# A Mamba stack with experts on one core: squares at the slot's end, powers moved, two banks for transposes, one for outputs

## The chip, the cores and the metric

The kernel runs on one core of a Trainium2 chip. The metric is the time of the kernel on the device in microseconds (us); lower is better. The core has five engines that work side by side, each through its own list of instructions in order: TensorE (PE in the profile, with PEld for its weight loads), VectorE (DVE), ScalarE (ACT), GpSimd (POOL) and SyncE (SP), which here issues most of the transfers. They wait for one another only where data or buffers ask for it.

## The reference

The input x has 8 sequences of 512 tokens with 128 channels, all in float32. A modulated LayerNorm is followed by four Mamba-2 layers, a gated residual, a second modulated LayerNorm, and a mixture of 8 experts (two per token) with a shared expert:

```python
h = _layernorm(x) * (1 + ca) + sa
for l in range(4):                      # Mamba-2 layer
    zxbcdt = rmsnorm(h) @ Wi            # z, xBC, dt
    xBC = silu(causal conv of 4 taps)   # xs, Bm, Cm
    dt = softplus(dt + dtb)
    hs = hs * exp(dt * A) + dt * xs * B ; y = hs @ C + D * xs
    h = h + rmsnorm(y * silu(z)) @ Wo
x = x + ga * rmsnorm(h)
h = _layernorm(x) * (1 + cb) + sb
x = x + gb * moe(h)                     # rmsnorm, router, top 2 of 8, plus shared expert
```

## The kernel before

The scan over tokens is done in chunks of 128. A *unit* is one sequence in one layer (32 units, `U`), an *item* is one chunk of a unit (128 items, `NI`, four to a unit). One loop over t runs all of it as a software pipeline. In slot t each stage works on another item; the slots of the loop are the order in which every engine gets its instructions, since the schedule inside is written by hand (`tc.manual_schedule`). For item i the stages are, with the slot in which they run and the engine:

- `decay_rows` (slot i-4, DMA), `decay_diff` and `decay_mask` (slot i-3, GpSimd, L793 and L798), `decay_exp` (slot i-2, ACT, L809): the decay matrix dV of the chunk, 128 x 1024;
- `transposes` (slot i-2): PE transposes the inputs into a PSUM bank called ptx (L828), and ACT copies them to xT (L830); `weigh` (slot i-1): GpSimd scales xT to xd and xe (L836, L839);
- `gram` (slot i-1): PE multiplies B and C (L848) into the last columns of the bank in which the next item's transposes land; `mix` (slot i): DVE multiplies dV by it (L852);
- `state_out` (slot i): PE, from the carried state (L861, L870); `state_decay` on GpSimd (L886), `state_next` on DVE (L895, L902);
- `chunk_out` (slot i+1): PE (L910, L920); `gate` (slot i+1): DVE multiplies by silu(z) to g (L932); `square` (slot i+1): ACT squares g for the norm (L936);
- `project_out` (slot i+2): PE sums the squares (L947) and projects g (L951) into a PSUM bank po that two items share; `out_scale` (slot i+2, odd i): DVE forms the mean (L958), GpSimd raises it to -1/2 (L959); `out_add` (slot i+3, odd i, so an even slot): DVE adds both chunks to the residual h (L967).

Sixteen slots ahead the same loop prepares the units: `project_x`, `project_z` and `project_dt` on PE (L638, L644, L682), four convolution taps per block of channels (ACT L650, then DVE L660 three times), `silu` on ACT in every fourth slot with a table load before and after it (L672, L673, then L809), and softplus on DVE (L706 to L740). `renorm` makes the next layer's input: squares on ACT (L155), a GpSimd power (L149, L150), scaling (hn, L203), transposes (L208) and a copy (hT, L210).

[...] Before, three serve the projections, one ptx, two py and two po.

When the last layer of a pair of sequences is done, `rejoin(g)` takes them (group g of four) through the final norm, the residual, the second LayerNorm, the second norm and the router. It is a generator: each `yield` ends a piece. In the drain, from slot 112 on, it is stepped twice in a slot. `mean_squares` squares on ACT and `power` takes the result to -1/2: on GpSimd in one instruction for groups 0 and 1 (`on_pool`), on DVE by a first guess from the bits and three Newton steps, 11 instructions, for groups 2 and 3. At its end each group has 16 scatters (GpSimd indirect DMAs, L488) that send rows to the experts' lists. After the loop, the shared expert (`serve`, L557, L535, with ACT's L524 and L528) is interleaved with the pieces that are left; then 39 expert tiles follow, and the final sums.

Of the kernel before, what the change touches and what calls it, by code (L numbers as in the profile page):

```python
# [11 lines left out]
ALU = mybir.AluOpType  # L12
AX = mybir.AxisListType
PSUM = bass.MemoryType.PSUM
# [10 lines left out]
def adaln_mamba_moe(  # L25
# [27 lines left out]
    nc = tc.nc  # L53
# [239 lines left out]
    def power(v, name, on_pool):  # L293

        n = v.shape[1]
        y = small.tile([P, G2], F32, tag="py", name=f"py{name}")[:, :n]
        if on_pool:
            nc.gpsimd.tensor_tensor(y, v, mhalf[:, :n], ALU.pow)
            return y
        t = small.tile([P, G2], F32, tag="pt", name=f"pt{name}")[:, :n]  # L300
        nc.vector.tensor_single_scalar(t.bitcast(I32), v.bitcast(I32), 1, ALU.arith_shift_right)
        nc.vector.tensor_scalar(y.bitcast(I32), t.bitcast(I32), -1, 0x5F3759DF, ALU.mult, ALU.add)
        for _ in range(3):
            nc.vector.tensor_mul(t, y, y)
            nc.vector.scalar_tensor_tensor(t, t, -0.5, v, ALU.mult, ALU.mult)
            nc.vector.scalar_tensor_tensor(y, t, 1.5, y, ALU.add, ALU.mult)
        return y

    def mean_squares(h, eps, name, on_pool):
        n = h.shape[1]  # L310
        ss = small.tile([P, G2], F32, tag="pss", name=f"pss{name}")[:, :n]
        for j in range(n):
            nc.scalar.activation(unread, h[:, j, :], AF.Square, accum_out=ss[:, j : j + 1])  # L313
            if j % NC == NC - 1:
                yield
        v = small.tile([P, G2], F32, tag="pv", name=f"pv{name}")[:, :n]
        nc.vector.tensor_scalar(v, ss, 1.0 / DM, eps, ALU.mult, ALU.add)
        return power(v, name, on_pool)

    def rejoin(g):  # L320
# [17 lines left out]
        mine = slice(b0 % 2 * NC, b0 % 2 * NC + n)  # L338
        h, xt = (v[b0 // 2].rearrange("p b s d -> p (b s) d")[:, mine] for v in (hp, xp))
        on_pool = g < 2  # L340
        rs = yield from mean_squares(h, 1e-5, f"F{g}", on_pool)
        yield
        for j in range(n):
            nc.scalar.activation(h[:, j, :], h[:, j, :], AF.Copy, scale=rs[:, j : j + 1])
# [14 lines left out]
            yield  # L359
        v = small.tile([P, G2], F32, tag="pv", name=f"pvL{g}")[:, :n]  # L360
        nc.vector.tensor_scalar_add(v, mv[:, :, 1], 1e-5)
        rs = power(v, f"L{g}", on_pool)
        if on_pool:
            yield
# [9 lines left out]
        for k in (2, 1):  # L374
            for t, m in both(k):
                nc.vector.tensor_tensor(h[:, t, :], h[:, t, :], m, ALU.mult if k == 2 else ALU.add)
            yield
        rs = yield from mean_squares(h, 1e-8, f"G{g}", on_pool)
        yield

        while scatters and scatters[0][0] in held.get(len(rowpools), [])[:-1]:
# [2 lines left out]
        rows = [rowpools[-1].tile([P, G2, RW], F32, tag=f"row{c}", name=f"row{c}_{g}")[:, :n] for c in range(2)]  # L384
        for j in range(n):
            nc.scalar.activation(rows[0][:, j, :DM], h[:, j, :], AF.Copy, scale=rs[:, j : j + 1])  # L386
            if j % NC == NC - 1:
                yield
        for c in range(2):
            nc.scalar.activation(rows[c][:, :, DM + 1], tok[:, :n], AF.Copy, bias=float(c * T + b0 * L))  # L390
        for i, b in enumerate(seqs):
# [94 lines left out]
    def scatter(to, of, ix, group):  # L486

        i = nc.gpsimd.indirect_dma_start(  # L488
            out=to, out_offset=bass.IndirectOffsetOnAxis(ap=ix, axis=0), in_=of, in_offset=None
        )  # L490
        tc.declare_no_dep(i.ins, group=group, reason="the rows that they write are distinct")
        tc.add_to_no_dep_group(group, i.ins)
# [80 lines left out]
    with ExitStack() as actx:  # L573
# [6 lines left out]
        w3 = actx.enter_context(tc.tile_pool(name="w3", bufs=3))  # L580
        df = actx.enter_context(tc.tile_pool(name="df", bufs=6))
        rows = actx.enter_context(tc.tile_pool(name="rows", bufs=3, space=bass.MemoryType.DRAM))
        psX = actx.enter_context(tc.tile_pool(name="psX", bufs=1, space=PSUM))
        psY = actx.enter_context(tc.tile_pool(name="psY", bufs=2, space=PSUM))
        psO = actx.enter_context(tc.tile_pool(name="psO", bufs=2, space=PSUM))

        U = NL * B
        NI = U * NC
# [345 lines left out]
        def square(i):  # L934
            sqs[i] = wk.tile([P, NB, Q], F32, tag="sq", name=f"sq{i}")
            nc.scalar.activation(sqs[i], gs[i], AF.Square)  # L936
# [18 lines left out]
        def out_scale(i):  # L955
            if i % 2:
                rs = small.tile([P, 2], F32, tag="rg", name=f"rg{i}")
                nc.vector.tensor_scalar(rs, po[i // 2][:, 2 * DM : 2 * DM + 2], 1.0 / DI, 1e-5, ALU.mult, ALU.add)  # L958
                nc.gpsimd.tensor_tensor(rs, rs, mhalf[:, 0:2], ALU.pow)  # L959
                po[i // 2] = po[i // 2], rs  # L960

        def out_add(i):
            if i % 2:
                pp, rs = po.pop(i // 2)
                for c in range(2):
                    b, s = i // NC % B, i % NC - 1 + c
                    nc.vector.scalar_tensor_tensor(  # L967
                        hs[b][:, s, :], pp[:, c * DM : (c + 1) * DM], rs[:, c : c + 1], hs[b][:, s, :], ALU.mult, ALU.add
                    )

        def item(i):
            return 0 <= i < NI

        def unit(v):
            return 0 <= v < U
# [17 lines left out]
        for t in range(-NC * LEAD - EARLY, NI + 4):  # L993
            p = t + NC * LEAD
            drain = p >= NI
            if p == 5 - EARLY:
                gens["small"] = load_small()
            if p == 0:
                gens["experts"] = prepare_experts(df)
            if p == 7 - EARLY:  # L1000
                gens["lists"] = clear_lists()
            if t == NI - LEAD * NC + 2:
                for k, w in enumerate((sw1, sw2.rearrange("(k p) o -> p k o", p=P))):
                    w12.append(wip.tile([P, NPROJ], F32, tag="Wi", name=f"ws{k}")[:, :FH])
                    dst = w12[k] if k == 0 else w12[k].rearrange("p (k o) -> p k o", o=DM)
                    nc.sync.dma_start(dst, w)
            for g, seqs in enumerate(sets):
                if t == NC * (U - B) + NC * (seqs[-1] + 1) + 2:
                    gens["pairs", g] = rejoin(g)
            v, j = divmod(p, NC)  # L1010
            vc, jc = divmod(p - 1, NC)

            if (p + 2 * NC) % (NC * B) == 0 and unit(p // NC + 2):
                load_weights((p // NC + 2) // B)
            if p % (NC * B) == NC and unit(v):
                scale_weights(v // B)
            if p == NC:
                nc.scalar.activation(negA, negA, AF.Exp)
                nc.scalar.mul(negA, negA, -1.0)
            if (p + EARLY) % NC == 0 and 0 <= (p + EARLY) // NC < B:  # L1020
                gens[(p + EARLY) // NC] = enter((p + EARLY) // NC)
            if t % NC == 3 and unit(t // NC - 1) and t // NC - 1 + B < U:
                gens[t // NC - 1 + B] = renorm(t // NC - 1)

            if item(t + 4):
                decay_rows(t + 4)
            vz, jz = divmod(p - 5, NC)
            if jz == 0 and unit(vz):
                silu(vz)
            if item(t + 2):  # L1030
                decay_exp(t + 2)

            if item(t):
                state_out(t)
            if item(t - 1):
                chunk_out(t - 1)
            if item(t):
                state_decay(t)
            if item(t + 1):
                weigh(t + 1)  # L1040
            if drain and scatters and item(t + 3):
                scatter(*scatters.pop(0)[1:])
            if item(t):
                mix(t)
            if item(t - 3):
                out_add(t - 3)
            if item(t):
                state_next(t)
            if drain:
                step_pairs()  # L1050
            if item(t - 1):
                gate(t - 1)
                square(t - 1)
            if item(t - 2):
                project_out(t - 2)
            if item(t + 1):
                gram(t + 1)
            if item(t + 2):
                transposes(t + 2)
            if item(t + 3):  # L1060
                decay_diff(t + 3)
                decay_mask(t + 3)
            if unit(vc):
                conv_tap(vc, jc, 1)
            if item(t - 2):
                out_scale(t - 2)
            if unit(vc):
                conv_tap(vc, jc, 2)
                conv_tap(vc, jc, 3)
                px.pop((vc, jc))  # L1070
            for key in list(gens):
                if not step(gens[key]):
                    del gens[key]
            if drain and routed:
                serve()
            group_stages(p, ((sums_a, 7),))
            if j == 1 and unit(v):
                project_dt(v)
            group_stages(p, ((softplus_a, 2), (softplus_b, 3), (softplus_c, 5), (softplus_d, 6), (sums_b, 7)))
            if unit(v):  # L1080
                project_x(v, j)
                conv_first(v, j)
            if j == 0 and unit(v - 1):
                project_z(v - 1)

# [244 lines left out]
```

## Time and profile before

| | |
|---|---|
| median of 3 runs | 1150.12 us (1149.14 to 1151.19) |
| the profiled execution | 1149.32 us, of it the span 1146.8 us |
| items 0 to 112 (starts of L852) | 94.26 to 744.24 us |
| drain and rest of the Mamba part | 744 to about 880 us |
| last group's norm and router, shared expert | 880 to 937 us |
| last scatters | 937 to 957 us |
| expert tiles | 961 to 1117 us |

How to read it: the profile is of one execution. "Busy" of an engine is the time that its instructions took; a group of instructions is a source line with an engine, and its row ends with the idle time of the engine just before them and what ended it. The costliest groups are L793 on POOL (128 times 1905 ns), L852 on DVE (128 times 1211 ns), L660 on DVE (384 times 745 ns) and L809 on ACT (128 times 1051 ns). The starts of consecutive instructions of one engine can overlap their durations a little[...].

The small operations that the change moves take: L936 square 414 ns (x128), L959 power 716 ns (x64), L967 addition 343 ns (x128, two in a row start 260 ns apart), L298 power of 8 columns 1.64 us (x6), L848 300 ns (x256), L947 256 ns (x512).

### The profile page before, as it was taken

How to read it: one execution, taken by the hardware profiler on the slowest of the kernel's cores; microseconds unless marked ns; L12 is line 12 of the kernel's file. 1: busy time of each engine (PE TensorE's matmuls, PEld its weight loads, DVE VectorE, ACT ScalarE, POOL GpSimd, SP SyncE). 2: the span in 40 equal slices, each digit the busy share in tenths (PEclk: the TensorE clock that was granted, in tenths of full speed). 3: DMA queues.
4: the chain of work that ended last, by engine and by line, in shares of the span. 5: the costliest groups of instructions: out<-in, count | busy, mean ns of one | idle time of the engine just before them, and what ended most of it. 6: DMA issues, size and time to landing. Idle time of an engine off the chain costs nothing. (4 is left out here: it accounts for less than half of the span.)

```text
span 1146.8 us, 21570 instructions
## 1 busy us (share of the span) xinstructions
PE 964.2 (84%) x7130; PEld 730.3 (64%) x7130; DVE 856.5 (75%) x2084; ACT 761.1 (66%) x1641; POOL 855.9 (75%) x937
## 2 busy tenths in 40 slices
PE   3666899989999889999998999879664994999995
PEld 1234666766677667666666676657453673988882
DVE  2767888798988988988889888887764652666653
ACT  3676888888898788888978887876534741333320
POOL 6858889798898898988988988989666163555550
PEclk9777989999999999999999999986886896999997
DMA  6964536443253243343332434434201016877756
GB/s 154 235 164 158 181 100 188 132 133 110 85 162 110 87 140 109 108 128 107 121 110 87 141 109 125 134 91 131 86 26 37 6 47 156 227 225 224 222 153 224
DMA packets 134303, 151.19 MB, mean 132 GB/s; under 512 B 22569, under 2 KB 106697, under 8 KB 134193
## 3 DMA queue, kind: packets, MB, share of 16 engines
q1 hardware_dynamic: 127184, 137.91, 41.1%
q0 software_dynamic: 4672, 9.42, 2.5%
q10 hardware_dynamic: 2336, 2.50, 0.7%
q8 instruction: 56, 0.92, 0.3%
q14 instruction: 55, 0.44, 0.1%
HBM read 120.07 MB, written 29.71 MB: 131 GB/s over the span
## 5 line engine op out<-in xcount | busy, mean ns | idle before, releaser
L660 DVE SCALAR_TENSOR_TENSOR xbc<-px,cw,xbc 128x511 f32<-128x511 f32 (+2 forms) x384 | 286.2, 745 | 23.4 <-ACT xbc L650 16.3
L793 POOL TENSOR_TENSOR dV<-dV,cum 128x1024 f32<-128x1024 f32 x128 | 243.8, 1905 | 5.4 <-DMA dV<-crow 5.3
L852 DVE TENSOR_TENSOR dV<-dV,ptx 128x1024 f32<-128x1024 f32 x128 | 155.0, 1211 | 18.7 <-ACT xT L830 18.6
L798 POOL TENSOR_SCALAR_AFFINE_SELECT dV<-dV 128x1024 f32<-128x1024 f32 x128 | 142.6, 1114 | 9.3
L809 ACT ACTIVATE dV<-dV 128x1024 f32<-128x1024 f32 x128 | 134.5, 1051 | 14.5 <-POOL dV L798 14.1
L488 POOL DMA_INDIRECT yg<-y,ix x78 | 84.1, 1078 | 77.5 <-DVE y L1216 62.9
L936 ACT ACTIVATE sq<-g 128x256 f32<-128x256 f32 x128 | 53.0, 414 | 119.0 <-DVE g L932 105.1
L638 PE MATMUL px<-hT,Wi 128*128 128x512 f32 x192 | 103.6, 621 | 15.9 <-DVE xbc L660 14.5
L650 ACT ACTIVATE xbc<-px,cbias,cw 128x512 f32<-128x512 f32 x128 | 98.4, 769 | 27.2 <-PE px L638 25.6
L488 POOL DMA_INDIRECT xg<-row,ix x64 | 63.3, 989 | 50.4 <-ACT hds L524 29.7
L836 POOL TENSOR_TENSOR xd<-xT,dt 128x256 f32<-128x256 f32 x128 | 79.2, 619 | 27.3 <-ACT xT L830 26.9
L861 PEld LDWEIGHTS py<-xbc,st 128*128 128x128 f32 x384 | 59.8, 202 | 60.1 <-issue 47.3
L951 PE MATMUL po<-Wo,g 128*128 128x128 f32 x512 | 88.9, 297 | 0.0
L1198 ACT ACTIVATE hd<-ph,bs 128x256 f32<-128x256 f32 x78 | 32.7, 470 | 84.3 <-PE ph L1192 81.9
L920 PE MATMUL py<-dV,xd 128*32 128x128 f32 x2048 | 84.5, 284 | 0.0
L947 PEld LDWEIGHTS po<-ones,sq 128*128 128x128 f32 x512 | 67.6, 192 | 26.1 <-issue 23.4
L910 PEld LDWEIGHTS py<-xbc,dg 128*128 128x128 f32 x512 | 79.5, 202 | 7.0 <-issue 1.0
L848 PE MATMUL ptx<-xbc 128*128 128x128 f32 x256 | 55.8, 300 | 33.1 <-DVE dV L852 32.4
L910 PE MATMUL py<-xbc,dg 128*128 128x128 f32 x512 | 81.9, 285 | 0.0
L947 PE MATMUL po<-ones,sq 128*128 128x1 f32 x512 | 78.1, 256 | 0.5 <-ACT sq L936 0.5
L1192 PE MATMUL ph<-xt,w 128*128 128x256 f32 x312 | 75.9, 388 | 0.1
L1205 PE MATMUL pe<-w,hd 128*128 128x128 f32 x624 | 75.9, 275 | 0.0
(252 smaller groups left out, 2343.0 us busy)
## 6 DMA issues: line engine op xcount, KB each, us to landing
dV<-crow SPq DMA_DIRECT2D x128, 512.0 KB, 3.8
w<-in_L_ffn_ew_dram SPq DMA_DIRECT2D x78, 256.0 KB, 3.5
xg<-blank SPq DMA_DIRECT2D x64, 260.0 KB, 5.9
ecum<-crow SPq DMA_DIRECT2D x256, 48.0 KB, 3.4
rows<-xg SPq DMA_DIRECT2D x39, 130.0 KB, 3.3
b<-in_L_ffn_eb_dram SPq DMA_DIRECT2D x39, 64.0 KB, 3.8
x<-in_L_attn_x_dram SPq DMA_DIRECT2D x8, 256.0 KB, 6.9
md<-mods SPq DMA_DIRECT2D x8, 256.0 KB, 4.9
```

Of the source, the lines that this page charges most:

```text
L488: i = nc.gpsimd.indirect_dma_start(out=to, out_offset=bass.IndirectOffsetOnAxis(ap=ix, axis=0), in_=of, in_offset=None)
L638: nc.tensor.matmul(px[v, k][:, :L], Wi[l][:, c0 : c0 + P], hT[v], start=True, stop=True)
L650: nc.scalar.activation(xbc[v][:, k, :], px[v, k][:, :L], AF.Identity, bias=cbias[:, l, k : k + 1], scale=cw[:, l, k, KT - 1 : KT],)
L660: nc.vector.scalar_tensor_tensor(xbc[v][:, k, d:], px[v, k][:, : L - d], cw[:, l, k, KT - 1 - d : KT - d], xbc[v][:, k, d:], ALU.mult, ALU ...
L793: nc.gpsimd.tensor_tensor(dV[i], dV[i], cums[g][:, h0 : h0 + NH].unsqueeze(2).to_broadcast([P, NH, Q]), ALU.subtract)
L798: nc.gpsimd.affine_select(out=dV[i], in_=dV[i], pattern=[[0, NH], [1, Q]], compare_op=ALU.is_ge, fill=-200.0, base=0, channel_multiplier=-1,)
L809: nc.scalar.activation(dV[i], dV[i], AF.Exp)
L852: nc.vector.tensor_mul(Ms[i], Ms[i], pg.pop(i).unsqueeze(1).to_broadcast([P, NH, Q]))
L910: nc.tensor.matmul(py[i][:, k, :], dg[l][:, k, :], xbc[u][:, k, t], start=False, stop=True, skip_group_check=True,)
L920: nc.tensor.matmul(py[i][j * HD : (j + 1) * HD, k, :], xd[:, h, :], M[:, h, :], start=False, stop=True, skip_group_check=True,)
L947: nc.tensor.matmul(pp[:, 2 * DM + c : 2 * DM + c + 1], sq[:, k, :], ones[:, 0:1], start=(k == 0), stop=(k == NB - 1))
L951: nc.tensor.matmul(pp[:, c * DM : (c + 1) * DM], g[:, k, :], Wo[l][:, k, :], start=(k == 0), stop=(k == NB - 1))
```

## The change

It has six parts.

1. `square(t - 1)` is issued at the end of slot t, after the norm work and the convolution's first tap, in place of right after `gate(t - 1)`.
2. `out_add(t - 3)` is issued before `mix(t)` in place of after it.
3. The pool for ptx gets two banks in place of one, the pool for po one in place of two.
4. `out_scale` calls `power`, so the result goes to a tile of its own; for the items 125 and 127 (`i < NI - 4` is false) it runs on DVE.
5. For groups 0 and 1 of `rejoin` there is a `yield` between the DVE instruction that forms the variance and the GpSimd power, three times.
6. The second norm's squares (`rest` is n in place of NC) and its scaled rows are issued for all chunks of the group in one piece, in place of two.

```diff
-    def mean_squares(h, eps, name, on_pool):
+    def mean_squares(h, eps, name, on_pool, rest):
...
-            if j % NC == NC - 1:
+            if j % rest == rest - 1:
                 yield
         v = small.tile([P, G2], F32, tag="pv", name=f"pv{name}")[:, :n]
         nc.vector.tensor_scalar(v, ss, 1.0 / DM, eps, ALU.mult, ALU.add)
+        if on_pool:
+            yield
         return power(v, name, on_pool)
...
-        rs = yield from mean_squares(h, 1e-5, f"F{g}", on_pool)
+        rs = yield from mean_squares(h, 1e-5, f"F{g}", on_pool, NC)
...
         nc.vector.tensor_scalar_add(v, mv[:, :, 1], 1e-5)
+        if on_pool:
+            yield
         rs = power(v, f"L{g}", on_pool)
...
-        rs = yield from mean_squares(h, 1e-8, f"G{g}", on_pool)
+        rs = yield from mean_squares(h, 1e-8, f"G{g}", on_pool, n)
...
             nc.scalar.activation(rows[0][:, j, :DM], h[:, j, :], AF.Copy, scale=rs[:, j : j + 1])
-            if j % NC == NC - 1:
-                yield
+        yield
...
-        psX = actx.enter_context(tc.tile_pool(name="psX", bufs=1, space=PSUM))
+        psX = actx.enter_context(tc.tile_pool(name="psX", bufs=2, space=PSUM))
         psY = actx.enter_context(tc.tile_pool(name="psY", bufs=2, space=PSUM))
-        psO = actx.enter_context(tc.tile_pool(name="psO", bufs=2, space=PSUM))
+        psO = actx.enter_context(tc.tile_pool(name="psO", bufs=1, space=PSUM))
...
-                nc.gpsimd.tensor_tensor(rs, rs, mhalf[:, 0:2], ALU.pow)
+                rs = power(rs, f"g{i}", i < NI - 4)
...
+            if item(t - 3):
+                out_add(t - 3)
             if item(t):
                 mix(t)
-            if item(t - 3):
-                out_add(t - 3)
...
                 gate(t - 1)
-                square(t - 1)
...
                 project_x(v, j)
                 conv_first(v, j)
+            if item(t - 1):
+                square(t - 1)
             if j == 0 and unit(v - 1):
                 project_z(v - 1)
```

## The prediction

> **What bounds the kernel now.** I read the page first, then its busy time by stretches of 50 us, the list of waits, and the timeline of single stretches; the chain of waits reaches back only to 879 us.
>
> ```profile
> PE 964.2 (84%) x7130; PEld 730.3 (64%) x7130; DVE 856.5 (75%) x2084; ACT 761.1 (66%) x1641; POOL 855.9 (75%) x937
> ...
> 500.00:550.00 50.00, 46.50 (x399) 35.50 (x398) 43.09 (x91) 43.07 (x85) 44.17 (x49) 1.00 0.41 132
> ```
>
> Columns of the second line: stretch, length, then busy us of PE, PEld, DVE, ACT and POOL, clock, DMA share, GB/s. In the steady part all four engines are busy for 86 to 93%. No engine alone is the bound: a loop of waits between them is. The starts of L852 repeat every 8 items to 0.01 us: item 70 at 503.99, item 78 at 549.21. I call these 45.22 us a lap; items 0 to 112 (94.26 to 744.24) are 14 laps.
>
> ```profile
> ACT sq L936 <- DVE g L932: 105.1, 76, 6.3
> DVE py L895 <- PE py L870: 36.6, 31, 2.6
> PE ptx L848 <- DVE dV L852: 32.4, 31, 6.0
> DVE dV L852 <- ACT xT L830: 18.6, 15, 1.9
> DVE h L967 <- POOL rg L959: 17.6, 7, 7.8
> ```
>
> (Who waited for whom: us in total, times, longest.) The change aims at the first and third. But where does the lap turn? In the lap from 503.99 DVE waits in only four places for over 0.3 us: 1.42 for xT of item 71 (ACT, behind silu), 1.03 and 1.28 at L895 of items 73 and 77 (PE, behind the pz matmuls), 0.42 for st; 4.2 us in all. ACT's long waits for g are mostly slack: at 534.73 it had waited 2.50 us, but L760 two steps on could not begin before DVE's L758, which ends at 537.25, and began at 537.61. Removing that wait is worth 0.36 us there, not 2.5.
>
> The end is different:
>
> ```profile
> 817.38 1.65 POOL L298 TENSOR_TENSOR pyG<-pvG,mhalf 128x8 f32<-128x8 f32 x1 [6.04 <-DVE pvG L317]
> ...
> 872.29 0.16 DVE L958 TENSOR_SCALAR rg<-po 128x2 f32<-128x2 f32 x1 [2.10 <-PE po L951]
> 880.25 0.61 DVE L967 SCALAR_TENSOR_TENSOR h<-po,rg,h 128x128 f32<-128x128 f32 x2 [7.80 <-POOL rg L959]
> ...
> 878.84 0.70 POOL L1111 IOTA tiles<- 128x312 f32 x1
> 879.48 0.74 POOL L959 TENSOR_TENSOR rg<-rg,mhalf 128x2 f32<-128x2 f32 x1
> ```
>
> The last norm's input is ready at 872.45; its power stands on GpSimd behind ten scatters (865.80 to 878.59) and two iotas. The chain that ended last starts just there, at 879.54, with that power and then L967.
>
> **The skill.** The Trainium skill's PSUM page (PSUM — Partial Sum Buffer, "PSUM bank collisions raise a hardware error") counts accesses of two engines to one bank at once as a collision, reads with reads included, so software has to order them. The trace agrees: mix (L852) at 503.99 starts when the xT copy of the next item ends (503.96), though they read different columns of the bank. Its page Perfetto Trace Analysis, "Optimization Strategy", takes repeated gaps as a hint at too few buffers; L848's wait for mix fits, but the trace prices it at 32.4 us in 31 of 128 slots only. Trainium Architecture — The Big Picture, "Inside one NeuronCore", gives each engine its own stream; 10 scatters in front of a 0.74 us power show what order within a stream costs.
>
> **The change, part by part.** t is the slot.
>
> *Two banks for ptx.* gram(t+1) no longer waits for mix(t). In the lap this frees PE by 0.47 (510.34) and 1.00 us (534.02).
>
> *One bank for po, additions first.* In even slots project_out now waits for both out_adds. DVE pays nothing in busy time (0.52 us moves ahead of mix), but mix now stands behind the GpSimd power. At 503.61 that power (0.69) ends at 504.30: out_add runs 504.34 to 504.95, mix starts at 504.86 instead of 503.99, and L895, which before came after both, starts at 506.00 instead of 505.65: 0.35 us late. In slot 72 softplus holds DVE to 515.09, so out_add ends at 515.70; PE could issue L947 at 514.9 and waits 0.8 us.
>
> *Squares at the end.* ACT's order becomes exp, xT, norm work, conv, sq. No work is added. After silu (slots 1 mod 4) sq now stands behind hn (1.18 us) and conv (0.67): it ends about 506.1, where before it ended at 503.70, and PE's L947 at 504.74 waits for it, 1.4 us. This is the new wait that I expect everywhere after slots with hn or the renorm squares. Queued behind L947 on PE are L951, gram, transposes and px; ACT's xT and conv and GpSimd's xd wait for those.
>
> I lay the longest loop of the new order with the trace's start-to-start times: from xT(71) over hn, conv and sq to L947(68) 2.55; to L947(69) 3.98 (po to px 1.55, px 0.86, state 0.45, dg 0.54, py 0.58); gram, transposes, hT 2.97; to L947(70) 2.56 (through px and through the squares alike); to L895(73) 5.32 (px 1.65, px and pz 2.58, L870 and its end 1.09); DVE from there to L758's end 16.06, as now; ct, conv, sq to L947(74) 1.71; px 2.61; conv, sq and the silu block to xT(79) 7.55 (the block alone 6.46). The sum is 45.31. The loop through GpSimd (edec, 11.2 us of unbroken GpSimd work to the power, out_add, DVE to pz, L895(73), L758) comes to 45.2. So a lap goes from 45.22 to about 45.3: 14 laps, +1.3 us, and I take +2 with a first lap that pays the 0.35. Unknown: some 30 hops of which each may be off by 0.03, that is up to 0.9 us a lap either way. Bounds: below, the wait that DVE has now, 4.2 us, cannot all go; I take -0.9 a lap (-13 us); above, +0.9 (+13 us).
>
> *GpSimd's powers a piece later; rows and squares whole.* Only groups 0 and 1. In the drain GpSimd waited 2.15 us for pvF at 764.9 and 6.04 for pvG at 817.38, with xd, xe, the difference and the mask queued behind. In the new order these go first. From 744 to 812 GpSimd is busy 60.9 of 68 us, so at most the 2.15 can be won. From 812 to 850 the xd is not the only thing late: DVE's L895 of item 123 waited 3.3 us at 821.70 for PE behind phs, which waited for ACT's hds, which stood behind sq waiting for g; with sq last that goes. Against it, a DVE power (2.3 us) now precedes the indices in program order, so the 16 scatters, GpSimd's bound until 848, start only about 1 us earlier. I take -4 us for 744 to 850 (bounds +3 and -10).
>
> *Last powers on VectorE.* Two powers of 11 small operations on DVE; the row of the same code (880.97 to 883.22) says 2.25 us. For item 125 it costs up to 2.2 us in a stretch where DVE has no gaps (852 to 862), where GpSimd took 0.69: +1.5. For item 127: 872.45 + 2.25 = 874.7, out_add at 874.75 instead of 880.25: -5.5. What is late next is the first wait in the rest of the chain, ACT's squares of group 3 and PE's shared experts; PE has about 13 idle us between 874 and 894, so it can follow. Group 3 also needs fewer pieces, so one phs pair (1.03 us) less stands before pos, and goes under the 20 us of scatters. Together -5 (bounds 0 and -9).
>
> The experts after 961 us and the start are as before; I count them as nothing (the start's slots are bounded by the same engines, up to 2 us either way).
>
> **Sum.** +2 - 4 - 5 = -7 us against the profiled execution's 1149.3 (span 1146.8 and 2.5 around it); the median of the runs shown, 1150.1, lies 0.8 above it. -7 from the median gives 1143.
>
> **Rivals.**
> - *The lap does shrink (1130).* For it: 105 us of ACT waiting and 32 us of PE waiting vanish, and the slack I see may be used by a loop I have not laid. Against: DVE's own waits, the lap's true cost, have other releasers. At -0.8 a lap, -11, and -9 at the end: 1130.
> - *The single po bank binds (1155).* One mechanism: out_add, first on DVE, waits for the GpSimd power, and PE's project_out waits for out_add, so DVE, GpSimd and PE meet in every even slot. For it: GpSimd runs unbroken from 538.35 to 570.9, and its power ends after DVE's slot is free (504.30 against 503.99). Against: DVE waits there today for xT anyway. Priced at +1.0 a lap, +14, less 9 at the end: 1155. It decides from about +0.65 a lap on, where the end's 9 us are used up.
> - *Both cancel (1150).* +9 in the laps against -9 at the end; or the end's 5.5 us are taken back by PE's queue of shared experts, continuously busy from 894 on, and the laps stay at +2.
>
> **How the numbers follow.** Balanced laps with a shorter end, 1136 to 1147: 0.48. The shrinking lap: 0.18. The bank that binds: 0.23. Cancelling: 0.11. The time is that of the first, 1143, its own range 1136 to 1147. To leave out no more than two in ten the range runs to 1130 and to 1156. Within 0.2% (2.3 us of 1150.1, about what this kernel's measurement can tell from no change) lies the cancelling case: faster 0.66, same 0.11, slower 0.23.
>
> **What would show it.** Right: ACT's wait for g in front of sq and PE's L848 wait for mix nearly gone; new waits of PE's po matmul for sq and for L967's out_adds; DVE's out_add waiting for the power in even slots; lap near 45.3; pyG's 6 us gone; the last out_add 1 to 2 us after its scale, and the first expert tile's rows some 9 us closer to the last lap. Wrong: a lap under 44.8 or over 45.8, or an end chain that still starts with a wait of several us for GpSimd.

## The result, and the profile after

The changed kernel takes 1156.58 us (median of 6 runs, 1155.44 to 1160.49) against 1149.63 us of the kernel before in the same comparison: 1.0067 times, 95% interval 1.0050 to 1.0085, some 7 us slower. A later comparison gave 1.0055 (1.0038 to 1.0072). The profiled execution has a span of 1153.7 us, 6.9 more than the 1146.8 before. In lines after the change, numbers above about 310 are 2 to 4 higher: mix is L855, the square L939, the sum of squares L950, the addition L970, and the power of the outputs now stands in L298. The level of the kernel before differed between comparisons (1148 to 1170 us), so every ratio below is to runs of before in its own comparison.

The list of waits of the kernel after, with the same columns as before:

```profile
ACT xT L833 <- PE ptx L831: 100.4, 93, 5.8
PE po L950 <- ACT sq L939: 42.6, 43, 2.4
DVE py L898 <- PE py L873: 37.3, 28, 3.3
DVE h L970 <- POOL pyg L298: 34.7, 18, 13.9
POOL pyg L298 <- DVE rg L961: 21.3, 22, 8.1
PE po L950 <- DVE h L970: 15.4, 5, 7.9
ACT sq L939 <- DVE g L935: 10.3, 3, 6.2
```

Each wait at which the change aimed is gone or nearly gone: ACT's for g fell from 105.1 to 10.3 us, and TensorE's wait of 32.4 us for mix (L848, now L851) no longer stands in the list. They came back elsewhere. ACT now waits 100.4 us for the transposes, TensorE 42.6 us for the squares, and VectorE's wait for GpSimd's power ahead of the additions doubled from 17.6 to 34.7 us.

In the stretch in which the kernel before had 46.50 us of TensorE and 44.17 us of GpSimd:

```profile
500.00:550.00 50.00, 45.55 (x373) 34.13 (x371) 42.46 (x88) 41.82 (x82) 43.75 (x49) 1.00 0.42 135
```

All four engines are busy for 0.4 to 1.3 us less of the 50: the steady part did not become denser. The 6.9 us, by the starts of mix, after against before:

| stretch | before | after | difference |
|---|---|---|---|
| start to item 0 | 94.3 | 94.9 | +0.7 |
| items 0 to 16 | 100.8 | 102.6 | +1.8 |
| three laps with a change of layer (from items 16, 48, 80) | 46.82, 46.82, 46.81 | 47.67, 47.66, 47.66 | +2.5 |
| eight ordinary laps up to item 104 | 45.21 to 45.22 | 45.27 to 45.28, two of 46.37 and 45.70 | +2.0 |
| items 104 to 127 | 161.9 | 161.2 | -0.7 |
| item 127 to the last addition | 21.4 | 20.7 | -0.7 |
| from there to the end | 266.3 | 267.5 | +1.2 |

Six of the eight ordinary laps are at 45.27 to 45.28. The two others are longer: in the one of 46.37 the slot that is 1.1 us longer falls into a stretch with a lower clock (last section); in the one of 45.70 one slot is 0.4 us longer at full clock, and why is open.

Not every row can be put down to the change, since profiles of the same instructions differ. Items 0 to 16 take 100.8 to 103.2 us in the six profiles in which nothing of the change acts there (before, e7, b1, b3, b4, g3 of the next section), so +1.8 shows nothing.

For items 104 to 127, e7 is the measure: up to the last two powers it has the instructions of the kernel before, in the same order on TensorE, VectorE, ScalarE and GpSimd, and it takes 157.5 us, not 161.9. The 4.4 us arise before item 125 (134.9 against 139.3 us from item 104). The largest piece is the slot from item 121 to 122, 12.01 us before and 8.01 in e7: before, TensorE's granted clock was 0.53 from 796 to 803 us, and in e7 it was 1.00 over the same instructions.

From the last addition to the end, the kernel after takes 267.5 us in one profile and 264.0 in another (c1). The laps, in contrast, mostly repeat to about 0.1 us from profile to profile where no stretch of lower clock falls into them. So what is shown to be the change's is +2.5 us where the layer changes and +0.5 in the ordinary laps, 3.0 of the 6.9 us.

The laps were expected to cost 2 us and the end to gain 9. The laps cost more, most of it where the layer changes, and no gain at the end is to be seen.

### The profile page after: what moved, and what is told of

It is laid out like the page before. It is cut to its first block, busy times and chain, and to the rows that moved or that the text cites. A ratio compares the mean times of both kernels' runs of the same rounds, so it can differ in the third digit from the quotient of the medians.

```text
span 1153.7 us, 21642 instructions
## 1 busy us (share of the span) xinstructions
PE 955.2 (83%) x7130; PEld 730.4 (63%) x7130; DVE 866.5 (75%) x2106; ACT 763.3 (66%) x1641; POOL 857.8 (74%) x935
## 4 chain that ended last, share of the span: by engine, by line
PE 29%; DVE 28%; POOL 21%; DMA 8%; ACT 6%; issue 6%; SPq 2%; POOLq 0%; ACTq 0%; DVEq 0%
DVE xbc L663 10%; POOL dV L796 6%; PE pe L1209 5%; DVE dV L855 5%; DMA rows<-xg 4%; PE ph L1196 3%; POOL dV L801 3%; PE px L641 3%; POOL xg L491 2%; POOL pyg L298 2%; PE pz L647 2%; DVE g L935 2%; POOL xd L839 2%; POOL xe L842 2%; PE py L923 2%
## 5 line engine op out<-in xcount | busy, mean ns | idle before, releaser
L855 DVE TENSOR_TENSOR dV<-dV,ptx 128x1024 f32<-128x1024 f32 x128 | 155.0, 1211 | 2.8 <-ACT xT L833 2.8
L950 PE MATMUL po<-ones,sq 128*128 128x1 f32 x512 | 79.1, 258 | 60.6 <-ACT sq L939 42.6
L950 PEld LDWEIGHTS po<-ones,sq 128*128 128x128 f32 x512 | 69.2, 196 | 90.1 <-ACT sq L939 65.6
L833 ACT COPY xT<-ptx 128x384 f32<-128x384 f32 (+1 forms) x128 | 57.4, 448 | 100.5 <-PE ptx L831 100.4
L864 PEld LDWEIGHTS py<-xbc,st 128*128 128x128 f32 x384 | 61.5, 204 | 65.9 <-issue 41.9
L954 PE MATMUL po<-Wo,g 128*128 128x128 f32 x512 | 91.4, 303 | 0.0
L864 PE MATMUL py<-xbc,st 128*128 128x128 f32 x384 | 63.2, 290 | 18.2 <-DVE rg L961 9.4
```

The costliest lines, as they stand in the source:

```text
L855: nc.vector.tensor_mul(Ms[i], Ms[i], pg.pop(i).unsqueeze(1).to_broadcast([P, NH, Q]))
L864: nc.tensor.matmul(py[i][:, k, :], st[i - 1][:, k * P : (k + 1) * P], xbc[u][:, NB + 1, t], start=(k == 0), stop=True, skip_group_check=True,)
L950: nc.tensor.matmul(pp[:, 2 * DM + c : 2 * DM + c + 1], sq[:, k, :], ones[:, 0:1], start=(k == 0), stop=(k == NB - 1))
```

## The experiments

All start-to-start times are from the profiles, in us; "lap" is the usual ordinary lap, "layer" one with a change of layer.

| kernel | parts of the change in it | lap | layer | items 104-127 | ratio to before, 95% |
|---|---|---|---|---|---|
| before | none | 45.22 | 46.81 | 161.9 | 1 |
| after, again (c1) | 1 to 6 | 45.27 | 47.63 | 162.4 | 1.0055 (1.0038-1.0072) |
| e8 | 2 | 45.56 | 48.0 | 164.5 | 1.0119 (1.0085-1.0153) |
| e6 | 1 | 45.66 and more | 46.78 | 159.6 | 1.0027 (1.0009-1.0045) |
| e3 | 1, 2, 4, 5, 6 | 45.42 | 47.9 | 161.3 | 1.0087 (1.0052-1.0121) |
| e2 | 1, 3, 4, 5, 6 | 48.06 | 47.6 to 50.3 | 161.1 | 1.0284 (1.0264-1.0303) |
| e4 | 2, 3, 4, 5, 6 | 45.57 | 47.96 | 162.0 | 1.0066 (1.0037-1.0094) |
| g4 | 1, 2, 3 | 45.26 | 47.62 | 166.3 | 1.0079 (1.0054-1.0104) |
| e1 | 1 to 4 | 45.28 | 47.66 | 166.4 | 1.0143 (1.0113-1.0172) |
| e5 | 1 to 6, power of item 123 on DVE | 45.27 | 47.66 | 158.8 | 1.0119 (1.0097-1.0141) |
| g1 | 1 to 6, powers from item 109 on DVE | 45.27 | 47.62 | 173.2 | 1.0220 (1.0162-1.0279) |
| g5 | 1 to 6, part 2 not in the drain | 45.26 | 47.62 | 161.7 | 1.0075 (1.0048-1.0103) |
| e7 | 4 | 45.20 | 46.81 | 157.5 | 0.9985 (0.9968-1.0002) |
| b1 | 4, 5, 6 | 45.22 | 46.86 | 160.2 | 0.9993 (0.9978-1.0008) |
| b3 | 4, and 1 in the drain alone | 45.22 | 46.85 | 159.5 | 0.9975 (0.9954-0.9995) |
| b4 | 4, 5, 6, and 1 in the drain alone | 45.22 | 46.86 | 161.8 | 0.9992 (0.9977-1.0007) |
| g3 | as b3, power of item 123 on DVE | 45.20 | 46.80 | 161.4 | 0.9968 (0.9951-0.9984) |

e1, e2, e4 and e5 were compared together at a level of 1165.7 us for before, and g1, g3, g4 and g5 at 1169.6; the others at 1148 to 1150. In the profiles of the first two comparisons the stretch from the last addition to the end takes 284 to 295 us, in the others 263 to 268, while the laps agree. So laps are compared between all kernels, and times best within one comparison. The column of items 104 to 127 is one profile each; a difference of up to 4.4 us in it between two single profiles shows nothing.

**The squares back (e4), the order back (e2).** The first theory was that additions ahead of mix let mix wait for GpSimd (A); its rivals, that the rejoin's later powers (B) or the late squares (C) do the harm.

```diff
 gate(t - 1)
+square(t - 1)
...
-if item(t - 1):
-    square(t - 1)
```

> The changed kernel with the squares right after the gate again (part 1 undone). Theory C: the waits of TensorE's L950 for the squares (42.6 us in 43 slots) go, ordinary laps drop under 45.0 us, time about 1151. Theories A and B: ordinary laps stay within 0.2 of 45.3, the stall of item 126 stays, time within 2 us of 1156.6.

The lap grows by 0.3 us to 45.57, more than the 0.2 that A and B allowed, and it does not fall below 45.0. C is refuted: inside the change the late squares gain in the laps. The time does not show this gain: 1.0066, where the change itself had 1.0067 and 1.0055.

```diff
-if item(t - 3):
-    out_add(t - 3)
 if item(t):
     mix(t)
+if item(t - 3):
+    out_add(t - 3)
```

> The changed kernel with out_add after mix again, all else kept (part 2 undone). Theory A: the laps with a layer change go back from 47.66 towards 46.8 us, mix of item 126 no longer waits 14 us for the power of item 123 (it starts before 852 instead of 859.6), time 1150 to 1152. Against it, TensorE's po bank waits a little longer for the additions: up to +0.3 us a lap, and if this binds the time stays at 1156. Theories B and C: within 1.5 us of 1156.6.

The lap rises to 48.06, where A had expected it to stay within 0.3 us: a miss. It explains why the parts belong together. With one output bank, project_out cannot start before the additions are through: for 29 of the 30 pairs from items 40 and 41 to 98 and 99, TensorE's sum starts 0.15 to 0.43 us after the end of the additions. e6 below has the same order and the same late squares, but two output banks, and its shortest lap is 45.66. So behind mix the single bank costs up to 2.4 us a lap, and the order of part 2 takes 2.8 us off again. Only this order makes part 3 bearable.

**One part at a time (e8, e6, e3).**

> The kernel before with out_add ahead of mix and nothing else of the change: two output banks, early squares. Theory A (the order alone makes mix wait for GpSimd's power): laps with a layer change 47.9 instead of 46.8, items 112 to 120 in 51 to 53 us instead of 48, ordinary laps within 0.3 of 45.2; time 1.004 to 1.008 of before. The rival (the order costs only where late squares make the output sums, and with them the power, late): laps 45.2 and 46.8, items 112 to 120 in 48, time 0.999 to 1.001.

```diff
+if item(t - 3):
+    out_add(t - 3)
 if item(t):
     mix(t)
-if item(t - 3):
-    out_add(t - 3)
```

A holds, with the order as the only edit: ordinary laps +0.34, layers +1.2 (47.94 and 48.07; the first was 49.31). The time, +1.2%, is above the 0.4 to 0.8% that A had forecast. The waits between 240 and 740 us, first before, then e8, then after, show the exchange:

```profile
DVE dV L852 <- ACT xT L830: 12.0, 9, 1.4
DVE h L967 <- POOL rg L959: 1.3, 2, 0.6
```

```profile
DVE h L967 <- POOL rg L959: 17.6, 10, 1.8
```

```profile
DVE h L970 <- POOL pyg L298: 15.2, 11, 1.8
PE po L950 <- DVE h L970: 4.1, 2, 2.1
```

Before, VectorE waited 12.0 us for xT ahead of mix and hardly at all for the power. With the additions first it waits for the power instead, 15 to 18 us, and mix and all behind it wait too. The price is highest where GpSimd is late. VectorE in a slot at a layer change, first before, then after:

```profile
412.84 1.21 DVE L852 TENSOR_TENSOR dV<-dV,ptx 128x1024 f32<-128x1024 f32 x1
414.69 0.61 DVE L967 SCALAR_TENSOR_TENSOR h<-po,rg,h 128x128 f32<-128x128 f32 x2 [0.64 <-POOL rg L959]
```

```profile
418.52 0.61 DVE L970 SCALAR_TENSOR_TENSOR h<-po,pyg,h 128x128 f32<-128x128 f32 x2 [1.77 <-POOL pyg L298]
419.04 1.21 DVE L855 TENSOR_TENSOR dV<-dV,ptx 128x1024 f32<-128x1024 f32 x1
```

Here GpSimd also makes the next layer's norm power, and its order puts that ahead:

```profile
411.73 0.19 POOL L149 TENSOR_SCALAR rr<-ss 128x4 f32<-128x4 f32 x1
412.00 1.04 POOL L150 TENSOR_TENSOR rr<-rr,mhalf 128x4 f32<-128x4 f32 x1
...
417.78 0.70 POOL L298 TENSOR_TENSOR pyg<-rg,mhalf 128x2 f32<-128x2 f32 x1
```

Before, mix went in front of the late power and was 1.2 us long itself; the additions then waited 0.64. After, mix stands behind it.

> The kernel before with the squares at the slot's end and nothing else of the change. If the 0.3 us a lap that undoing the squares cost in the changed kernel is the squares' own worth, an ordinary lap is 44.9 instead of 45.22 and the time 0.996 of before. If the squares help only in company with the single output bank, laps stay at 45.2 or grow, since TensorE's sums then wait for ACT after silu and hn: 1.000 to 1.006 of before.

```diff
-square(t - 1)
...
+if item(t - 1):
+    square(t - 1)
 if j == 0 and unit(v - 1):
     project_z(v - 1)
```

The second branch came true: alone the late squares cost at least 0.44 us a lap. TensorE's sum waits for them there, 24.2 us between 240 and 740 us, but in the kernel after it waits 28.7 us in the same stretch and the late squares gain, so this wait alone does not settle the cause. Items 104 to 127 take 159.6 us against 161.9; since e7, with early squares, takes 157.5, a gain of the late squares in the drain is not shown.

> The changed kernel with one bank for the transposes and two for the outputs again; additions still ahead of mix. Theory A (the order: an addition that waits for GpSimd's power holds mix): laps with a layer change stay at 47.7, items 112 to 120 stay near 51 us, and the lap gains nothing or pays up to 0.3 us for TensorE's wait for mix; time 1.005 to 1.010 of before. Theory D (the single output bank, which lets TensorE wait for the additions and so for GpSimd): laps with a layer change go back to 46.8, ordinary ones to 45.0, items 112 to 120 to 48; time 0.995 to 1.001 of before.

```diff
-psX = actx.enter_context(tc.tile_pool(name="psX", bufs=2, space=PSUM))
+psX = actx.enter_context(tc.tile_pool(name="psX", bufs=1, space=PSUM))
...
-psO = actx.enter_context(tc.tile_pool(name="psO", bufs=1, space=PSUM))
+psO = actx.enter_context(tc.tile_pool(name="psO", bufs=2, space=PSUM))
```

Layers stay at 47.9 and the lap at 45.42: A, not the single bank (D). Once the additions are first, the exchange of banks gains 0.15 us a lap. The list before had named TensorE's wait for mix as 32 us; the Trainium skill (Perfetto Trace Analysis, "Optimization Strategy") reads such a repeated gap as a hint at too few buffers. The gap went, and 0.15 us of a lap with it.

**The drain and the last powers (e1, g4, e5, g5, g1, e7, b1).**

> The changed kernel with the rejoin's extra pieces and whole rows undone (parts 5 and 6). Theory A (the additions now stand first on VectorE, so a late GpSimd power stops mix and all behind it): the 16 scatters of group 0 still stand ahead of the power of item 123, so mix of item 126 still waits over 10 us behind an addition; time within 1.5 us of 1156.6. Theory B (the powers a piece later do the harm: pyG of group 1 stands behind the output power of item 121 and the scatters start late): first scatter about 829 instead of 832.65 us, items 112 to 120 back from 51.0 to about 48, time about 1152. Theory C (the squares at the slot's end do the harm): no change.

> The changed kernel with parts 4, 5 and 6 undone, so squares, additions and banks alone. If parts 4 to 6 gain some 1 to 3 us inside the changed kernel, as parts 4 to 6 do alone on the kernel before (0.9993): 1.006 to 1.008 of before. If they lose there: below 1.005.

The edits take parts 5 and 6 (e1) and parts 4 to 6 (g4) out of the changed kernel:

```diff
-if on_pool:
-    yield
...
-rs = power(rs, f"g{i}", i < NI - 4)
+nc.gpsimd.tensor_tensor(rs, rs, mhalf[:, 0:2], ALU.pow)
```

B is refuted: in e1 items 112 to 120 take 50.8 us, not 48. A was not right about e1 either: it expected a wait of over 10 us ahead of the addition of item 122 and an unchanged time, and the wait shrank to 6.61 us while the ratio was 1.0143.

Without the later powers items 104 to 127 take 166.3 and 166.4 us, with them 161.1 to 162.4 in six profiles (after, c1, e2, e3, e4, g5). So in these stretches parts 5 and 6 gain 4 to 5 us inside the change, and parts 1 to 3 had cost about that much there first: 4.4 us from 161.9 to 166.3, or 8.8 from e7's 157.5. The level is not it: e4 and g5, from the same comparisons as e1 and g4, take 162.0 and 161.7.

The times do not agree on the gain: e1 is slower than e4 of its comparison (1.0143 against 1.0066), but g4 is level with g5 of its own (1.0079 against 1.0075). On the kernel without parts 1 to 3, parts 5 and 6 seem to lose 2.3 to 2.7 us (e7 to b1, b3 to b4), less than two profiles of the same instructions differ.

VectorE in the drain of the kernel after, at the longest wait of the list:

```profile
843.92 0.15 DVE L961 TENSOR_SCALAR rg<-po 128x2 f32<-128x2 f32 x1
...
859.07 0.61 DVE L970 SCALAR_TENSOR_TENSOR h<-po,pyg,h 128x128 f32<-128x128 f32 x2 [13.95 <-POOL pyg L298]
859.60 1.21 DVE L855 TENSOR_TENSOR dV<-dV,ptx 128x1024 f32<-128x1024 f32 x1
```

GpSimd meanwhile, from the scale on, issues the scatters of group 0; the last of them and the power:

```profile
857.32 0.96 POOL L491 DMA_INDIRECT xg<-row,ix  x1 [0.30 <-issue]
858.30 0.74 POOL L298 TENSOR_TENSOR pyg<-rg,mhalf 128x2 f32<-128x2 f32 x1
```

GpSimd's list is written by hand only inside the loop; after it a planner orders this one engine (`tc.manual_schedule(engines={*tc.nc.engines} - {mybir.EngineType.Pool})`, L1224), and it moves the scatters that are left over forward, between the loop's own instructions. In the trace all 16 stand ahead of the power of item 123. Scatters at 1.26 us each (844.81 to 846.08) stand in front of a power of 0.74 us whose input was ready at 844.07. In the kernel before the same 16 stood there too:

```profile
849.80 1.01 POOL L488 DMA_INDIRECT xg<-row,ix  x1 [0.17 <-issue]
850.84 0.73 POOL L959 TENSOR_TENSOR rg<-rg,mhalf 128x2 f32<-128x2 f32 x1
```

But the scale came late anyway (846.57), and the addition at 851.60 waited 2.72. Counted from the mix of item 112, the scale is 7.8 us earlier after the change and the last scatter 2.3 us later. This comes with parts 5 and 6, not with parts 1 to 3: from this scale to its addition b1, which has parts 4 to 6 alone, takes 14.8 us and b4 15.2, and e1 and g4, which have parts 1 to 3 but not 5 and 6, take 7.8.

> The changed kernel with the power of item 123 on VectorE as well, so that no output power stands behind group 0's scatters. Theory A: VectorE's wait of 13.95 us ahead of the additions of items 122 and 123 shrinks to under 3 us, mix of item 126 starts before 852 us, and the rest of the drain follows by half or more: time 1149 to 1153. Theory B: the stall goes but the end of the drain is set by the late scatters, time within 1.5 us of 1156.6. Theory C: the same as B.

> The changed kernel with out_add after mix from slot 112 on, ahead of it before. Theory A for the drain: mix of item 126 is no longer held behind the additions of items 122 and 123, items 112 to 120 in 48 to 49 us, 112 to 127 in at most 113 us: 1.002 to 1.004 of before. Rival: TensorE's single output bank takes the wait over and the drain stays as long, 116 us: 1.0055.

> The changed kernel with the output powers of all items from 109 on computed on VectorE instead of 125 and 127 alone. Theory A (mix waits for additions that wait for GpSimd's queue): VectorE's waits for pyg in the drain go (16.5 us between 744 and 862 in the changed kernel), items 112 to 127 take at most 112 us instead of 116.0; VectorE pays 2.3 us for each of six more powers, of which half lie in its idle time: time 1.001 to 1.004 of before. Rival (VectorE's own work binds the drain, so the power's place does not matter): 112 to 127 in 116 us or more, 1.006 or above.

```diff
-rs = power(rs, f"g{i}", i < NI - 4)
+rs = power(rs, f"g{i}", i < NI - 5)
```

That is e5; g1 has NI - 20 there, and g5 puts out_add behind mix where `drain` is true.

Off GpSimd (e5), the addition of item 122 starts 4.6 us after the scale instead of 15.2, and items 120 to 127 take 61.5 us instead of 65.0. The time that A had forecast from this did not come: 1.0119, where e4 of the same comparison has 1.0066. From the last addition to the end e5's profile takes 295.2 us and e4's 285.2; why is open. With mix first in the drain (g5) the wait stays, behind mix instead of ahead of it:

```profile
846.20 1.18 DVE L855 TENSOR_TENSOR dV<-dV,ptx 128x1024 f32<-128x1024 f32 x1
861.44 0.61 DVE L970 SCALAR_TENSOR_TENSOR h<-po,pyg,h 128x128 f32<-128x128 f32 x2 [14.06 <-POOL pyg L298]
```

The slot of 20.5 us is then that of item 127 instead of 126, and 104 to 127 take 161.7: A's claim for the drain, that the order costs there, is refuted inside the change. All drain powers on VectorE (g1) make it 173.2 us: it is busy for 119.67 of the 138 us from 744 to 882. So in these slots the place of this one power behind the scatters costs about 3.5 us, which no time shows, and moving all of them does harm.

> The kernel before with the output powers of items 125 and 127 on VectorE and nothing else of the change. My first theory: the last additions come 5.5 us earlier against mix of item 127 and about 4 of them reach the end: 0.996 of before. The rival, from the trace of the changed kernel (scale to addition 5.06 us there, not the 2.4 expected, and the scale itself 2.2 us later against mix): under 1 us is gained, 0.999 to 1.001.

> The kernel before with the last output powers on VectorE, the rejoin's powers a piece later and its squares and rows in one piece (parts 4, 5 and 6), nothing of parts 1 to 3. From e1 against the changed kernel parts 5 and 6 gain about 2 us between items 120 and 127; against this the last addition stands behind one more power on VectorE (2.35 us, as in the changed kernel). Theory: 0.996 to 0.9985 of before, and the last addition 4.5 to 5 us after its scale. Rival: parts 5 and 6 take back what part 4 gains, 1.000 or above.

```diff
-nc.gpsimd.tensor_tensor(rs, rs, mhalf[:, 0:2], ALU.pow)
+rs = power(rs, f"g{i}", i < NI - 4)
```

The last scale and additions of VectorE, in e7, then in the kernel after:

```profile
871.92 0.16 DVE L958 TENSOR_SCALAR rg<-po 128x2 f32<-128x2 f32 x1 [2.38 <-PE po L951]
...
874.28 0.61 DVE L967 SCALAR_TENSOR_TENSOR h<-po,pyg,h 128x128 f32<-128x128 f32 x2
874.81 0.36 DVE L317 TENSOR_SCALAR pvG<-pssG 128x8 f32<-128x8 f32 x1
```

```profile
880.82 0.16 DVE L961 TENSOR_SCALAR rg<-po 128x2 f32<-128x2 f32 x1 [1.21 <-PE po L954]
...
883.53 0.16 DVE L317 TENSOR_SCALAR pvG<-pssG 128x8 f32<-128x8 f32 x1
...
885.88 0.60 DVE L970 SCALAR_TENSOR_TENSOR h<-po,pyg,h 128x128 f32<-128x128 f32 x2
```

Alone, part 4 does what was worked out from the scale to the addition: 2.36 us, the forecast's 2.4. From the mix of item 127 to the last addition it gains 3.7 us (17.7 against 21.4) and not 5.6, since the scale itself comes 1.9 us later against that mix. Whether this reaches the end is not shown: the ratio of 0.9985 lies between the two forecasts, and its interval includes 1. In the change the way from the scale to the addition takes 5.06 us, since part 6 makes group 2's rejoin one piece earlier, and its own VectorE power (pvG, 883.53 to 885.96) falls between the two. b1 has the same 5.05 us (875.11 to 880.16), without parts 1 to 3; its time, 0.9993, is nearer to the rival's.

**A better version (b3, b4, g3).**

> The kernel before with the last output powers on VectorE (part 4) and the squares at the slot's end in the drain alone, from slot 112 on. If the late squares are good in the drain and bad in the laps: ordinary laps 45.2, items 112 to 120 in 46.3 us, 120 to 127 under 64 us; time about 0.995 of before. Rival: the gain between 112 and 127 is not passed on, because the scatters or the expert part bind: 0.9985, as with part 4 alone.

> The last kernel with parts 5 and 6 of the change as well. If all these gains add: 0.993 of before. Rival: parts 5 and 6 put one more power ahead of the last addition and cost 2 us against the last kernel: 0.997.

> The kernel before with late squares in the drain and the output powers of items 123, 125 and 127 on VectorE. The addition of item 123 no longer stands behind 16 scatters (scale to addition about 2.5 us instead of 5), and if the second LayerNorm of the last group follows it: 0.996 of before. Rival: mix goes first there anyway, nothing waits for the addition, and VectorE pays 2.3 us: 0.9975 to 0.9985.

```diff
-nc.gpsimd.tensor_tensor(rs, rs, mhalf[:, 0:2], ALU.pow)
+rs = power(rs, f"g{i}", i < NI - 4)
...
 gate(t - 1)
-square(t - 1)
+if not drain:
+    square(t - 1)
...
+if drain and item(t - 1):
+    square(t - 1)
```

That is b3 against before; g3 has NI - 5, b4 parts 5 and 6 as well. b3 keeps the laps at 45.22 and is 0.9975 of before; g3 has the lowest ratio, 0.9968 (0.9951 to 0.9984). Both lie below before with their whole interval, and below the kernel after, which was measured in another comparison. Where the gain comes from is not shown. In b3 items 112 to 120 take 47.1 us and 120 to 127 64.5, more than its theory asked for; from item 112 to 127 it takes 111.6 us, and so does e7 (111.5) without the late squares. The intervals of b3, g3 and e7 (part 4 alone) overlap. In g3 the way from the scale of item 123 to its addition is 5.76 us, not 2.5: the power on VectorE takes longer there, and mix goes first. b4 misses both its forecasts: its median of 1147.96 us against 1143.54 of b3 in the same comparison speaks against parts 5 and 6 in this kernel, though their intervals overlap too.

## Why the prediction was wrong

The sum was -7 us, to 1143; measured are +7, to 1156.58.

**What bounds the lap: right in size, the loop not shown.** The loop was laid at 45.31 us for the whole change; the ordinary lap measures 45.27 to 45.28. The prediction itself allowed 0.9 us either way, so agreement this close is in part luck. And the loop that it laid runs through the late squares, but without them (e4) the lap is not shorter; it is 0.3 us longer. The new waits came as named: TensorE's sum behind the late squares, VectorE's additions behind the power. So did the vanishing of ACT's wait for g at almost no gain. "DVE waits there today for xT anyway" holds in the ordinary laps of the whole change; with the order alone they pay 0.34 us (e8).

**"14 laps, +1.3": the step that failed first.** It laid one kind of lap and multiplied it. Three of the laps up to item 104 contain a change of layer, where GpSimd is later and that argument no longer covers the wait: +0.85 us each, not +0.1. The prediction's own figures contained the hint: from 94.26 to 744.24 us, 14 laps are 46.43 us each, not 45.22.

**"I take -4 us for 744 to 850": the larger failure.** In the profiles the gain of parts 5 and 6 was about that size inside the change (g4 and e1 against after: 4 to 5). But nothing was put into the sum for what parts 1 to 3 do to the drain, and in the profiles they cost 4.4 us or more (g4). So items 104 to 127 take 161.2 us after, against 161.9 and 157.5 for the same instructions before. Two details failed as well. The 16 scatters were to start "about 1 us earlier"; they start at 832.65 instead of 824.07, and counted from the mix of item 112 still 3.4 us later. And it was not asked which output power stood behind them: the addition of item 122 then waited 13.95 us. The wait of 6.04 us for pvG was to go, with xd and xe going first. GpSimd then waited longer, for the scale of item 121, and xd (831.28) still stands behind:

```profile
829.00 0.70 POOL L298 TENSOR_TENSOR pyg<-rg,mhalf 128x2 f32<-128x2 f32 x1 [8.14 <-DVE rg L961]
829.67 1.64 POOL L298 TENSOR_TENSOR pyG<-pvG,mhalf 128x8 f32<-128x8 f32 x1
```

**"-5" for the last powers: right alone from scale to addition, mis-sized in company.** The 5.5 us for item 127 rested on 2.25 us of power right after the scale. e7 has it: 2.36 us from scale to addition instead of 7.96, though its time does not show that the end gets it. In the change 2.4 us of another group's power stand between, and from item 127 to the last addition only 0.7 us are gained.

**The rivals.** The one called "the single po bank binds" was nearest in time (1155 against 1156.6), and half its mechanism is shown: additions wait for GpSimd's power. But it hardly binds in ordinary laps (+0.06 where it was priced at +1.0), and where it does it is not through the bank (e3: layers stay at 47.9 with two). That its time came near is luck: it put +14 us into the laps and -9 into the end, and the runs show neither. Its other half, TensorE behind the additions, is what e2 shows at 2.8 us a lap, which the order of part 2 averts.

Not settled: where the part of the 7 us comes from that the laps do not show, what in the drain parts 1 to 3 make slower, why the late squares gain with parts 2 to 6 and cost alone, and why parts 5 and 6 gain with parts 1 to 3 and not without them.

## What to carry to other kernels

Lay the loop for every kind of lap, not for the commonest: an in-order engine whose new first instruction waits for another is safe only while that other is early, and the rare laps are where it is late. Before a stretch of one profile is credited to a part, see how much it differs between profiles of the same instructions: here 157.5 and 161.9 us for one drain, but 0.1 us for a lap. When parts of a change act on the same stage, price each part there, also those made for another stage. An instruction of 0.7 us that moves to another engine is worth its wait only if nothing of that engine's own list slips in ahead of what it serves.

## What the runs showed of the hardware

TensorE's granted clock dips in the middle of steady laps, in most profiles, at changing places. In the records each dip lasts 3.4 us, a few twice that, at 0.50 of the full clock, and a slot in which one falls can get 1.1 to 1.7 us longer (7.24 against 6.14 us from item 42 to 43 after, at 347.04 to 354.28). Three windows around that slot, after; the clock is the first number behind the engines:

```profile
340.00:343.50 3.50, 3.50 (x36) 2.79 (x35) 2.34 (x5) 3.47 (x5) 3.43 (x5) 1.00 0.27 76
...
346.50:350.70 4.20, 4.20 (x33) 3.32 (x32) 3.18 (x8) 3.47 (x9) 3.57 (x3) 0.68 0.00 0
350.70:354.50 3.80, 3.80 (x40) 3.00 (x39) 3.56 (x11) 2.38 (x4) 2.20 (x3) 1.00 0.46 142
```

The Trainium skill (TensorE: Matmul & The Clock Gate, "What's actually happening") lets the clock fall after an idle stretch of about 3.4 us. Here the fall came at 345.77 us. TensorE was busy throughout the first window, and from 334 us to the fall it waited 0.45 us at most, so that reading does not cover it. One long lap in a profile is no evidence for a change.

The dips may all the same be part of what the change costs. Between the mixes of items 16 and 104 the profiles without parts 1 to 3 (before, e7, b1, b3, b4, g3) have 0 to 3 of them. The profiles with all three (after, c1, e1, g1, g4, g5, e5) have 3 to 7; the two of the changed kernel itself have 3 and 6 and lose 1.1 and 3.8 us by them in these laps. With one or two of parts 1 to 3 there are 2 (e4, e6), 5 (e8), 6 (e3) and 9 (e2). In the comparison of g1, g3, g4 and g5 there is 1 dip without parts 1 to 3 (g3) and there are 6 or 7 with them, so the level of a comparison is not the reason. What brings the dips is open; no run was made for it.

A VectorE operation on 128 x 2 values that takes 0.17 us in e7 (L302 at 872.31) took 0.58 us after (881.22 to 881.80), while GpSimd ran an iota from 881.11 to 881.77; in b1 it took 0.57. The Trainium skill (SBUF — State Buffer, "SBUF: two separate sides") gives the two engines a pair of ports in common, which for some kinds of VectorE operation one of them holds for a whole instruction. The end 0.03 us after the iota's fits that, but which kind this operation is no run shows. If it is so, an engine can be held up by another where neither data nor buffers ask for it.
